# A two-layer block on one core: negated maxima, a later moments' copy, later subtractions, weight products from split operands

## The chip, the cores and the metric

The kernel runs on one core of one Trainium2 chip. The metric is the device time of one execution in microseconds; the median of three runs is given. TensorE (PE) multiplies matrices, VectorE (DVE), ScalarE (ACT) and GpSimd (POOL) work on elements, SyncE (SP) issues the DMAs. PEld is PE's loading of weights, recorded beside its products.

## The reference

The input x holds 4 batches of 512 tokens with 256 features. Each of two layers computes a mixing part s and a gate g from the same normalised input and adds their product:

```python
xn = layernorm(x)
x  = x + s(xn) * silu(ffn(xn))
```

The feed-forward part of both layers is `fwht(silu(xn @ W1.T) * (xn @ W3.T)) @ W2.T` with 1024 hidden features; `fwht` is a Walsh-Hadamard transform along them. In layer 0, s is a recurrence of one step from a zero state, so it is linear: `xn + rmsnorm(xn @ W_in.T * c @ W_out.T) * norm_w`, with c per channel. In layer 1, s is causal attention with one head: a second layernorm with gamma and beta, q, k, v, softmax of `q k.T / 16`, the product with v, an output projection, and xn added.

## The kernel before, in words

Products that must keep fp32's accuracy are made of split operands: `split` (L59 to L62) copies a tile to a rounded high part on ACT (type float32r, "f32r") and subtracts it from the original on DVE to get a low part. `mm3` (L80 to L87) then adds three products: high by high, high by low, low by high. So each split costs one ACT and one DVE instruction, and PE runs f32r products. A few products of weights run in native fp32 instead: `product_of_weights` (L179) makes M, the 256x256 mixing matrix of layer 0 (tile mps), the product wqk of the query and key weights divided by 16 (tile wqkps), and the product wvo of the value and output weights (tile wvops). In a trace a native product of 256 columns is two records.

The kernel treats one batch after another, first all four in layer 0, then all four in layer 1. A scheduler sets the order on each engine from costs and dependences; `after(ins)` adds a constraint that an instruction comes behind another.

Layer 0. The FFN of a batch (`ffn`, L450) goes through eight hidden blocks c of 128: the up products of W1 and W3 (tile f_0gu for batch 0: the digit in f_0 is the batch), silu on ACT (L511), the product h on DVE (L512), the split of h into hh and hl (L519), and the down product of an earlier block (tile f_0dn). Beside it a list of tasks is stepped through slots (`Beside`, L850), two per block: the mixer, the norm of the next batch, and preparations. For batch 0 all down products are deferred to the end, so the split h of blocks 0 to 3 are kept in tiles "early", and the weights still have to be loaded and split beside it (w from w13raw, w2 by `prep_w2` at L139, M by `prep_m`). Batch 1 has among its tasks W2 of layer 1 and `prep_second`, which loads qk and vo and makes wqk and wvo.

`prep_s` (L311) prepares a quarter of layer 1's up weights for a form of Strassen's product with seven products for eight: it loads sraw, makes four sums on DVE (ssum), splits both into sp, and stores them to DRAM in four DMAs. `load_s` (L334) loads them back as tiles sw whenever the FFN of layer 1 (`ffn_s`, L536) needs them, into the four slots of w13. The stores and loads are issued by SP in its own order, like all large transfers. Tiles of 512 KB share ten slots (t4, L44): sraw, ssum, sp, qk, vo, the split q k product tq, v, p and the moments.

Layer 1. `norm(1, b)` (L416) computes the layernorm of batch b, then the moments of a second one (`moments`, L240), transposes them on PE (tile mrp), copies the 8 rows on ACT (L431), writes them to DRAM (L433) and loads them back, broadcast to all partitions, as mrb (L435). `Attention` (L711) makes tq (L757) from the scaled input and wqk, v from wvo, and the scores sc (L775) for four tiles of 128 rows. For each tile the mask is added on DVE (L792), a maximum taken (nmax, L794) and multiplied by -1 (neg, L796). `soft` (L798) makes the four exponentials p on ACT with neg as bias (L807). The first of a batch is preceded by a load of ACT's function table, since silu was used before. `pt` (L814) transposes p on PE in three groups (tiles 0 and 1, tile 2, tile 3) and splits it into ph and pl; `pv` (L828) multiplies by v. In layer 1 the order of PE is written out by hand: a list `places` (from L1058 on) says which attention step goes beside which of the FFN's products.

Of the kernel before, what the change touches and what calls it, by code (L numbers as in the profile page):

```python
# [35 lines left out]
def kernel(ctx: ExitStack, tc: tile.TileContext, a: dict, out: bass.AP):  # L36
# [139 lines left out]
    def w2_tiles(layer):  # L176
        return w2_tile(f"w2h_{layer}"), w2_tile(f"w2l_{layer}")

    def product_of_weights(name, lhsT, rhs, nk, scale=None):  # L179
# [9 lines left out]
        if scale is None:  # L189
            split(o, hi, lo)  # L190
        else:
            nc.scalar.mul(hi, o, scale)
            nc.vector.scalar_tensor_tensor(lo, o, scale, hi.bitcast(F32), ALU.mult, ALU.subtract)
        return hi, lo

    def load_m():
# [24 lines left out]
    def sl(i):  # L221
        return slice(i * P, (i + 1) * P)
# [3 lines left out]
        nc.sync.dma_start(raw, a[name])  # L226
        return raw

    def prep_qk(qk):
        return product_of_weights(  # L230
            "wqk", lambda k, i: qk[:, 0, k, sl(i)], lambda k: qk[:, 1, k, :], 2, 1.0 / 16.0
        )

    def prep_vo(vo):
        return product_of_weights(
            "wvo", lambda k, i: vo[:, 0, k, sl(i)], lambda k: vo[:, 1, k, :], 2
        )


    def moments(name, x, mr):  # L240
# [175 lines left out]
    def norm(layer, b):  # L416
        xn = act.tile([P, NT, D], F32, tag="xn", name=f"xn{layer}_{b}", bufs=3)
        xns[layer, b] = xn
        with after(first["gate"] if b > 1 - layer else None):
            first["scaled"] = layernorm(f"ln{layer}_{b}", xs[b], xn)  # L420
        yield
        if layer:


            mr = act.tile([P, 2, NT], F32, tag="mr", name=f"mr{b}", bufs=2)
            moments(f"ln2_{b}", xn, mr)
            yield
# [3 lines left out]
            nc.scalar.copy(rows, o)  # L431
# [3 lines left out]
            nc.sync.dma_start(  # L435
                mrb, there.rearrange("(a t) p -> a (t p)", a=2).unsqueeze(0).to_broadcast([P, 2, S])
            )
# [12 lines left out]
    def ffn(name, xT, w13, w2, slot, defer=1, spare=(), parts=1, behind=False, tail=()):  # L450
# [30 lines left out]
                        ins = one(False)  # L481
            return ins

        queue, gates = [], []
        for c in range(NH):
            with after(gates[-2] if behind and c >= 2 else None):
                wh, wl = w13(c // 2)
            gu = []
            for j in range(2):

                o = psum(f"{name}gu{c}_{j}", [P, S], **(DN[0] if behind and c == 1 else GU))
                cols = slice((c % 2) * D + j * P, (c % 2) * D + (j + 1) * P)
                gu.append((o, cols))
            for half in range(parts if c == 0 else 1):
                n = S // (parts if c == 0 else 1)
                ts_ = slice(half * n, (half + 1) * n)
# [15 lines left out]
            gates.append(nc.vector.tensor_tensor(h, h, gu[1], ALU.mult))  # L512
            first["gate"] = gates[-1]
            if c < len(spare):
                hh, hl = spare[c]
            else:
                hh = hid(f"{name}hh{c}", F32R)
                hl = hid(f"{name}hl{c}", F32R)
            split(h, hh, hl)  # L519
            queue.append((c, hh, hl))  # L520
            ups = last_up if behind else None
            with after(gates[-1] if behind else None), after(ups):
                slot(2 * c)
            if len(queue) > defer:
# [186 lines left out]
    class Attention:  # L711
# [63 lines left out]
        def sc(self, i):  # L775

            b = self.b
            if i == 0:
                self.both = psum(f"sc{b}_0", [P, 2, 2 * P])
                self.scs = [self.both[:, 0, :], self.both[:, 1, :]]  # L780
                self.nmax, self.neg, self.den = (
                    act.tile([P, NT], F32, tag=n, name=f"{n}{b}", bufs=2) for n in ("nmax", "neg", "den")
                )
            elif i > 1:
                self.scs.append(psum(f"sc{b}_{i}", [P, S]))
# [5 lines left out]
            for t in ones:  # L791
                nc.vector.tensor_tensor(self.scs[t][:, sl(t)], self.scs[t][:, sl(t)], mask, ALU.add)  # L792
            for t in ones:
                nc.vector.reduce_max(self.nmax[:, t : t + 1], self.scs[t][:, : (t + 1) * P], AX.X)  # L794
            ts_ = slice(ones[0], ones[-1] + 1)
            nc.vector.tensor_scalar(self.neg[:, ts_], self.nmax[:, ts_], -1.0, None, ALU.mult)  # L796

        def soft(self):  # L798

            b, ins = self.b, first["table"]  # L800
            self.ps, self.prs = [], []
            ps_ = [t4(f"p{b}_{i}", [P, 2, S]) for i in range(2)]
            for i, sc in enumerate(self.scs):
                w = (i + 1) * P
                p = ps_[i // 2][:, i % 2, :]
                with after(ins):
                    ins = nc.scalar.activation(  # L807
                        p[:, :w], sc[:, :w], AF.Exp,
# [41 lines left out]
    class Beside:  # L850
# [24 lines left out]
        def finish(self):  # L875
            while self.step():
                pass

    def some(gen, n):

        for _ in range(n):
            next(gen)
            yield

    def run(f, *args):
        return lambda: f(*args)
# [73 lines left out]
    def prep_second():  # L960
        qk, vo = load_pair("qk"), load_pair("vo")
        yield
        first["wqk"] = prep_qk(qk)
        yield
        first["wvo"] = prep_vo(vo)
        yield


# [1 line left out]
    for b in range(B):  # L970
# [8 lines left out]
        if b + 1 < B:  # L979
            if b:  # L980
                load_x(b + 1)
            if b == 2:
                tasks.append((prep_s(1), 4))
            tasks.append((norm(0, b + 1), NORM))
        if b == 0:
            early = w2_tile("early0"), w2_tile("early1")
# [4 lines left out]
        if b == 1:  # L991
            raw2_1 = load_w2(1)
            w2_1 = w2_tiles(1)
            tasks.append((prep_w2(1, raw2_1, w2_1, t4), W2P))
            tasks.append((prep_second(), 3))
            tasks.append((prep_s(0), 4))
        if b == 2:
            tasks += [(prep_s(2), 4), (norm(1, 0), NORM), (prep_s(3), 4)]
        if b == 3:
            atts = [Attention(0)]  # L1000
            a = atts[0]
            parts = run(a.xt_half, 0), run(a.xt_half, 1), a.xt, a.scaled, a.split_sums
# [43 lines left out]
    for b in range(B):  # L1046
        a, final = atts[b], b + 1 == B
        sc, pv, v = ([run(f, i) for i in range(NT)] for f in (a.sc, a.pv, lambda i: a.v(i // 2, i % 2)))
        pts = [run(a.pt, *tiles) for tiles in ((0, 1), (2,), (3,))]
        adds, later_gates = {}, [lambda: None] * 2  # L1050
        if b:
# [7 lines left out]
        else:  # L1059
            places = [[[v[0]], [v[1]], [v[2]], [sc[0]], [], [sc[1]], [v[3]], []]]  # L1060
        if not final:
            if b:
                places[0][2].append(run(next, norms[b + 1]))
            rows = run(next, norms[b + 1])
            c = Attention(b + 1)
            tq, v_ = [run(c.tq, j) for j in range(2)], [run(c.v, 0, j) for j in range(2)]
            atts.append(c)
            places += [
                [
                    [sc[2]], [sc[3], rows, a.soft], [0], [pts[0]],  # L1070
                    [1, later_gates[0]], [pts[1], later_gates[1]], [2], [pv[0], pv[1], 3],
                ],
                [
# [9 lines left out]
        else:  # L1083
            later = [[(q, c, (2, 3)) for c in range(2)] for q in range(2)]
            places += [
                [[sc[2]], [sc[3], a.soft], [0], [pts[0]], [1, later_gates[0]], [pts[1], later_gates[1]], [], [pv[0], pv[1]]],
                [[pts[2]], [pv[2], 0], [], [pv[3]], [1], [later[0][0]], [], [later[0][1]]],
                [[later[1][0]], [later[1][1]], [], [0], [], [1], [], []],
            ]
# [69 lines left out]
```

## Time and profile before

| what | us |
|---|---|
| median of three runs (lowest, highest) | 364.55 (364.49, 364.83) |
| the profiled execution | 364.85 |
| span of its trace | 363.0 |
| PE busy, PEld busy | 354.9, 327.3 |
| DVE busy, ACT busy, POOL busy | 283.9, 195.7, 20.5 |
| DMA: bytes moved | 52.25 MB |

The granted clock of TensorE is 1.00 throughout. The profile names tiles without buffer numbers: sw stands for all of sw0_0_0, sw0_1_1 and so on, where the text needs the number (sw0_1_1 is the high part of the second load, for quarter 1). Line L70 is `in_line`, the helper that records every matmul, so matmuls are told apart by their tiles. A row of a chain is start, length, engine, tile, line and count; a row of a timeline has besides, in brackets, the idle time before it and who ended it. As matmuls overlap in a pipeline, the duration of one (0.28 us for 256 columns) is longer than the distance between two starts.

### The profile page before, as it was taken

What the parts mean: (1) busy time and instruction counts of PE and PEld (TensorE: products, weight loads), DVE (VectorE), ACT (ScalarE), POOL (GpSimd) and SP (SyncE); (2) the same over time, 40 slices, a digit from 0 to 9 for tenths busy, and PEclk for the clock granted to TensorE, in tenths of its full rate; (3) what the DMA queues carried; (4) which work ended last, traced back from release to release, by engine and by line L of the source; (5) the groups of instructions that cost most, each with busy time, mean ns of one, the idle gap of its engine ahead of it and who ended that gap; (6) DMA issues with size and microseconds to landing.
All of it is one profiled execution on the core that took longest, in us unless ns stands there. A gap on an engine that the chain in (4) does not pass through costs nothing.

```text
span 363.0 us, 6253 instructions
## 1 busy us (share of the span) xinstructions
PE 354.9 (98%) x2461; PEld 327.3 (90%) x2461; DVE 283.9 (78%) x602; ACT 195.7 (54%) x370; POOL 20.5 (6%) x22
## 2 busy tenths in 40 slices
PE   8999999999999999999999999999999999999995
PEld 6867998888988898888989999899999899999995
DVE  6898548997569938897787957979669898568646
ACT  3647526265373424663467655577653876446443
POOL 1000201000020210101100001100011000000000
PEclk9999999999999999999999999999999999999999
DMA  7924200414235416633057145662554645345401
GB/s 242 327 61 148 87 0 2 128 46 178 84 127 179 159 27 218 259 121 105 1 209 255 33 171 205 225 204 95 202 201 144 197 188 202 114 148 212 194 2 58
DMA packets 16285, 52.25 MB, mean 144 GB/s; under 512 B 1633, under 2 KB 7937, under 8 KB 16257
## 3 DMA queue, kind: packets, MB, share of 16 engines
q1 hardware_dynamic: 15968, 51.60, 40.1%
q8 instruction: 19, 0.31, 0.4%
q10 hardware_dynamic: 288, 0.26, 0.2%
q14 instruction: 10, 0.07, 0.1%
HBM read 42.40 MB, written 9.45 MB: 143 GB/s over the span
## 4 chain that ended last, share of the span: by engine, by line
PE 80%; DVE 15%; ACT 1%; issue 1%; DMA 1%; POOL 1%; DVEq 0%
PE f_1gu L70 6%; PE f_2gu L70 6%; PE f_3gu L70 6%; PE f_3dn L70 6%; PE f_2dn L70 6%; PE f_0dn L70 5%; PE f_1dn L70 5%; PE f_0gu L70 4%; PE pv L70 4%; PE tq L70 3%; PE o L70 3%; PE v L70 2%; PE sc L70 2%; PE mps L70 1%; PE pt L70 1%; DVE nmax L794 1%
## 5 line engine op out<-in xcount | busy, mean ns | idle before, releaser
L70 PE MATMUL f_0gu<-xt,w 128*128 128x512 f32 (+1 forms) x108 | 25.3, 383 | 0.6 <-DVE f_0h L512 0.5
L70 PE MATMUL f_3gu<-xt,w 128*128 128x512 f32 x96 | 25.0, 396 | 0.0
L70 PE MATMUL f_2gu<-xt,w 128*128 128x512 f32 x96 | 24.6, 395 | 0.0
L70 PE MATMUL f_1gu<-xt,w 128*128 128x512 f32 x96 | 24.5, 395 | 0.0
L70 PEld LDWEIGHTS f_0gu<-xt,w 128*128 128x128 f32 x108 | 18.3, 188 | 6.1 <-DVE f_0h L512 0.9
L70 PEld LDWEIGHTS f_1gu<-xt,w 128*128 128x128 f32 x96 | 17.2, 188 | 3.3
L70 PEld LDWEIGHTS f_2gu<-xt,w 128*128 128x128 f32 x96 | 17.1, 188 | 3.2
L70 PEld LDWEIGHTS f_3gu<-xt,w 128*128 128x128 f32 x96 | 17.0, 188 | 2.9
L61 ACT CAST f_1hh<-f_1h 128x512 fp32r<-128x512 f32 x16 | 9.9, 621 | 16.6 <-DVE f_1h L512 12.3
L61 ACT CAST f_2hh<-f_2h 128x512 fp32r<-128x512 f32 x16 | 9.9, 621 | 15.6 <-DVE f_2h L512 11.2
L70 PE MATMUL f_1dn<-w2l,f_1hh 128*128 128x256 f32 x64 | 17.9, 284 | 0.0
L70 PE MATMUL f_3dn<-w2l,f_3hh 128*128 128x256 f32 x64 | 17.7, 281 | 0.0
L70 PE MATMUL f_1dn<-w2h,f_1hh 128*128 128x256 f32 x64 | 17.7, 281 | 0.0
L70 PE MATMUL f_3dn<-w2h,f_3hh 128*128 128x256 f32 x64 | 17.7, 281 | 0.0
L70 PE MATMUL f_2dn<-w2h,f_2hh 128*128 128x256 f32 x64 | 17.7, 282 | 0.0
L70 PE MATMUL f_2dn<-w2l,f_2hh 128*128 128x256 f32 x64 | 17.6, 280 | 0.0
L70 PE MATMUL f_1dn<-w2h,f_1hl 128*128 128x256 f32 x64 | 17.3, 284 | 0.1
L70 PE MATMUL f_3dn<-w2h,f_3hl 128*128 128x256 f32 x64 | 17.0, 282 | 0.0
L70 PE MATMUL f_2dn<-w2h,f_2hl 128*128 128x256 f32 x64 | 16.8, 283 | 0.1
L61 ACT CAST f_3hh<-f_3h 128x512 fp32r<-128x512 f32 (+1 forms) x17 | 10.1, 596 | 12.1 <-DVE f_3h L512 7.9
L62 DVE TENSOR_TENSOR f_2hl<-f_2h,f_2hh 128x512 fp32r<-128x512 f32 x16 | 11.0, 686 | 4.8 <-ACT f_2hh L61 4.8
L62 DVE TENSOR_TENSOR f_3hl<-f_3h,f_3hh 128x512 fp32r<-128x512 f32 (+1 forms) x17 | 11.1, 656 | 3.6 <-ACT f_3hh L61 3.3
(469 smaller groups left out, 1137.9 us busy)
## 6 DMA issues: line engine op xcount, KB each, us to landing
sw<-s SPq DMA_DIRECT2D x32, 896.0 KB, 4.7
s<-sp SPq DMA_DIRECT2D x8, 512.0 KB, 3.4
s<-sp SPq DMA_DIRECT2D x8, 384.0 KB, 4.3
w2raw<-in_w SPq DMA_DIRECT2D x4, 512.0 KB, 6.3
sraw<-in_w SPq DMA_DIRECT2D x4, 512.0 KB, 4.6
mrb<-there SPq DMA_DIRECT2D x4, 512.0 KB, 3.9
w13raw<-in_w SPq DMA_DIRECT2D x3, 512.0 KB, 8.4
x<-in_x SPq DMA_DIRECT2D x3, 512.0 KB, 3.5
```

The source lines that it names most:

```text
L61: h = nc.scalar.copy(hi, src)
L62: return h, engine.tensor_tensor(lo, src, hi.bitcast(F32), ALU.subtract)
L70: ins = call(*args, **kwargs)
L794: nc.vector.reduce_max(self.nmax[:, t : t + 1], self.scs[t][:, : (t + 1) * P], AX.X)
```

## The change

It has five parts.

1. The maxima are written negated straight into neg; the tile nmax and the multiplication by -1 go (12 DVE instructions).
2. `soft` is cut into halves. `places` has the first half, the moments' copy, then the second half, and the copy is put behind the last exponential by `after`.
3. In batch 0 of layer 0 the blocks 0 to 3 make only the high part hh at once. The four subtractions for hl are collected in `late` and issued behind the products h of the blocks 6 and 7, two each.
4. wqk and wvo are made from split operands: qk and vo are split as whole tiles, and `product_of_pair` uses `mm3`. `prep_second` has five steps in place of three.
5. `prep_s` of quarters 0, 1, 2 moves from batches 1, 2, 2 to batch 2 in other places, and that of quarter 3 from batch 2 to batch 3. The first two steps of norm(1, 1) move from the tasks of batch 3 to layer 1: the layernorm to its start, the moments to the place where the other batches have them.

```diff
-    def prep_qk(qk):
-        return product_of_weights(
-            "wqk", lambda k, i: qk[:, 0, k, sl(i)], lambda k: qk[:, 1, k, :], 2, 1.0 / 16.0
-        )
...
+    def split_pair(name, raw):
+        parts = [t4(f"{name}{i}", [P, 2, 2, D], F32R) for i in "hl"]
+        split(raw, *parts)
+        return parts
+
+    def product_of_pair(name, parts, scale=None):
...
+        for i in range(2):
+            mm3(
+                o[:, i, :],
+                [
+                    (tuple(p[:, 0, k, sl(i)] for p in parts), tuple(p[:, 1, k, :] for p in parts))
+                    for k in range(2)
+                ],
+            )
...
-            nc.scalar.copy(rows, o)
+            with after(first["table"] if b else None):
+                nc.scalar.copy(rows, o)
...
-            split(h, hh, hl)
+            if c < len(spare):
+                nc.scalar.copy(hh, h)
+                late.append((hl, h, hh))
+            else:
+                split(h, hh, hl)
+            for _ in range(2 if c >= NH - 2 else 0):
+                if late:
+                    lo_, h_, hi_ = late.pop(0)
+                    with after(gates[-1]):
+                        nc.vector.tensor_tensor(lo_, h_, hi_.bitcast(F32), ALU.subtract)
...
-                nc.vector.reduce_max(self.nmax[:, t : t + 1], self.scs[t][:, : (t + 1) * P], AX.X)
-            ts_ = slice(ones[0], ones[-1] + 1)
-            nc.vector.tensor_scalar(self.neg[:, ts_], self.nmax[:, ts_], -1.0, None, ALU.mult)
+                nc.vector.reduce_max(
+                    self.neg[:, t : t + 1], self.scs[t][:, : (t + 1) * P], AX.X, negate=True
+                )
...
-        first["wqk"] = prep_qk(qk)
-        yield
-        first["wvo"] = prep_vo(vo)
+        qk = split_pair("qk", qk)
+        yield
+        vo = split_pair("vo", vo)
+        yield
+        first["wqk"] = product_of_pair("wqk", qk, 1.0 / 16.0)
+        yield
+        first["wvo"] = product_of_pair("wvo", vo)
...
             if b == 2:
-                tasks.append((prep_s(1), 4))
+                tasks.append((prep_s(0), 4))
             tasks.append((norm(0, b + 1), NORM))
...
-            tasks.append((prep_second(), 3))
-            tasks.append((prep_s(0), 4))
+            tasks.append((prep_second(), 5))
         if b == 2:
-            tasks += [(prep_s(2), 4), (norm(1, 0), NORM), (prep_s(3), 4)]
+            tasks += [(prep_s(1), 4), (norm(1, 0), NORM), (prep_s(2), 4)]
...
             norms = {1: norm(1, 1)}
-            tasks.append((some(norms[1], 2), 2))
+            tasks.append((prep_s(3), 4))
...
-            if b:
-                places[0][2].append(run(next, norms[b + 1]))
+            if b == 0:
+                next(norms[1])
+            places[0][2].append(run(next, norms[b + 1]))
...
-                    [sc[2]], [sc[3], rows, a.soft], [0], [pts[0]],
+                    [sc[2]], [sc[3], soft[0], rows, soft[1]], [0], [pts[0]],
```

More of the change, by code (lines that the diff above doesn't have):

```diff
@@ L177, in w2_tiles, with product_of_weights @@
         return w2_tile(f"w2h_{layer}"), w2_tile(f"w2l_{layer}")
-    def product_of_weights(name, lhsT, rhs, nk, scale=None):
+    def product_of_weights(name, lhsT, rhs, nk):
         hi = wp.tile([P, 2, D], F32R, name=f"{name}h")
@@ L188, in product_of_weights @@
                 )
[L189 to L193, printed above, removed]
+        split(o, hi, lo)
         return hi, lo
@@ L227, in load_pair @@
         return raw
-    def prep_qk(qk):
-        return product_of_weights(
-            "wqk", lambda k, i: qk[:, 0, k, sl(i)], lambda k: qk[:, 1, k, :], 2, 1.0 / 16.0
-        )
[L234 to L237, printed above, removed]
+    def split_pair(name, raw):
[3 more added lines that the diff above has]
+    def product_of_pair(name, parts, scale=None):
+        hi = wp.tile([P, 2, D], F32R, name=f"{name}h")
+        lo = wp.tile([P, 2, D], F32R, name=f"{name}l")
+        o = psum(f"{name}ps", [P, 2, D])
+        for i in range(2):
[6 more added lines that the diff above has]
+            )
+        if scale is None:
+            split(o, hi, lo)
+        else:
+            nc.scalar.mul(hi, o, scale)
+            nc.vector.scalar_tensor_tensor(lo, o, scale, hi.bitcast(F32), ALU.mult, ALU.subtract)
+        return hi, lo
     def moments(name, x, mr):
@@ L482, in down @@
             return ins
-        queue, gates = [], []
+        queue, gates, late = [], [], []
         for c in range(NH):
@@ L518, in ffn @@
                 hl = hid(f"{name}hl{c}", F32R)
-            split(h, hh, hl)
+            if c < len(spare):
+                nc.scalar.copy(hh, h)
+                late.append((hl, h, hh))
+            else:
+                split(h, hh, hl)
[4 more added lines that the diff above has]
+                        nc.vector.tensor_tensor(lo_, h_, hi_.bitcast(F32), ALU.subtract)
             queue.append((c, hh, hl))
@@ L780, in sc @@
                 self.scs = [self.both[:, 0, :], self.both[:, 1, :]]
-                self.nmax, self.neg, self.den = (
-                    act.tile([P, NT], F32, tag=n, name=f"{n}{b}", bufs=2) for n in ("nmax", "neg", "den")
+                self.neg, self.den = (
+                    act.tile([P, NT], F32, tag=n, name=f"{n}{b}", bufs=2) for n in ("neg", "den")
                 )
@@ L793, in sc, with soft @@
             for t in ones:
-                nc.vector.reduce_max(self.nmax[:, t : t + 1], self.scs[t][:, : (t + 1) * P], AX.X)
-            ts_ = slice(ones[0], ones[-1] + 1)
-            nc.vector.tensor_scalar(self.neg[:, ts_], self.nmax[:, ts_], -1.0, None, ALU.mult)
-        def soft(self):
+                nc.vector.reduce_max(
+                    self.neg[:, t : t + 1], self.scs[t][:, : (t + 1) * P], AX.X, negate=True
+                )
+        def soft(self, h):
             b, ins = self.b, first["table"]
-            self.ps, self.prs = [], []
-            ps_ = [t4(f"p{b}_{i}", [P, 2, S]) for i in range(2)]
-            for i, sc in enumerate(self.scs):
+            if h == 0:
+                self.ps, self.prs = [], []
+            half = t4(f"p{b}_{h}", [P, 2, S])
+            for i in (2 * h, 2 * h + 1):
+                sc = self.scs[i]
                 w = (i + 1) * P
-                p = ps_[i // 2][:, i % 2, :]
+                p = half[:, i % 2, :]
                 with after(ins):
@@ L877, in finish @@
                 pass
-    def some(gen, n):
-        for _ in range(n):
-            next(gen)
-            yield
     def run(f, *args):
@@ L994 @@
             tasks.append((prep_w2(1, raw2_1, w2_1, t4), W2P))
-            tasks.append((prep_second(), 3))
-            tasks.append((prep_s(0), 4))
+            tasks.append((prep_second(), 5))
         if b == 2:
-            tasks += [(prep_s(2), 4), (norm(1, 0), NORM), (prep_s(3), 4)]
+            tasks += [(prep_s(1), 4), (norm(1, 0), NORM), (prep_s(2), 4)]
         if b == 3:
             atts = [Attention(0)]
-            a = atts[0]
-            parts = run(a.xt_half, 0), run(a.xt_half, 1), a.xt, a.scaled, a.split_sums
+            at = atts[0]
+            parts = run(at.xt_half, 0), run(at.xt_half, 1), at.xt, at.scaled, at.split_sums
             tasks += [(call(f), 1) for f in parts]
             norms = {1: norm(1, 1)}
-            tasks.append((some(norms[1], 2), 2))
+            tasks.append((prep_s(3), 4))
         bg = Beside(*tasks)
@@ L1048 @@
         sc, pv, v = ([run(f, i) for i in range(NT)] for f in (a.sc, a.pv, lambda i: a.v(i // 2, i % 2)))
+        soft = [run(a.soft, i) for i in range(2)]
         pts = [run(a.pt, *tiles) for tiles in ((0, 1), (2,), (3,))]
@@ L1085 @@
             places += [
-                [[sc[2]], [sc[3], a.soft], [0], [pts[0]], [1, later_gates[0]], [pts[1], later_gates[1]], [], [pv[0], pv[1]]],
+                [[sc[2]], [sc[3], *soft], [0], [pts[0]], [1, later_gates[0]], [pts[1], later_gates[1]], [], [pv[0], pv[1]]],
                 [[pts[2]], [pv[2], 0], [], [pv[3]], [1], [later[0][0]], [], [later[0][1]]],
```

## The prediction, made before the result was known

> **What bounds the kernel now.** I read the page first: the share of each engine and the chain that ended last.
>
> ```profile
> PE 354.9 (98%) x2461; PEld 327.3 (90%) x2461; DVE 283.9 (78%) x602; ACT 195.7 (54%) x370; POOL 20.5 (6%) x22
> ...
> PE 80%; DVE 15%; ACT 1%; issue 1%; DMA 1%; POOL 1%; DVEq 0%
> ```
>
> PE sets the end. An edit gains only by taking away matmul time or a place where PE stands still, and loses only where it makes PE stand. The waits of PE by name are next (engine, tile and line, who was late; us in total, times, longest).
>
> ```profile
> PE warm L70 <- DVE zr L904: 1.4, 1, 1.4
> PE pt L70 <- ACT p L807: 1.4, 3, 0.5
> PE f_0gu L70 <- DVE f_0h L512: 0.5, 1, 0.5
> PE xt_0tp L70 <- DVE xn L390: 0.2, 1, 0.2
> PE f_0gu L70 <- DVE w L62: 0.2, 1, 0.2
> ```
>
> Three of these five touch the change: the transposes of p (three times) and the two f_0gu waits. The table of stretches shows where they lie (length, then busy us of PE, PEld, DVE, ACT, POOL).
>
> ```profile
> 20.00:30.00 10.00, 9.36 (x37) 6.36 (x36) 10.00 (x18) 4.84 (x10) 0.00 (x0) 1.00 0.34 105
> 30.00:40.00 10.00, 10.00 (x54) 8.67 (x53) 7.59 (x18) 5.62 (x11) 0.00 (x0) 1.00 0.44 158
> 60.00:80.00 20.00, 20.00 (x115) 17.32 (x114) 19.17 (x40) 9.34 (x19) 2.77 (x2) 1.00 0.26 79
> 160.00:180.00 20.00, 20.00 (x139) 18.55 (x138) 14.79 (x40) 8.83 (x15) 2.39 (x2) 1.00 0.26 90
> 180.00:190.00 10.00, 9.53 (x73) 8.97 (x72) 8.14 (x21) 6.10 (x15) 0.00 (x0) 1.00 0.52 186
> 230.00:240.00 10.00, 9.46 (x70) 8.69 (x69) 10.00 (x24) 7.11 (x17) 1.27 (x1) 1.00 0.80 286
> 280.00:290.00 10.00, 9.44 (x76) 8.80 (x75) 8.54 (x20) 7.65 (x16) 0.00 (x0) 1.00 0.72 230
> ```
>
> PE is short of full at 20 to 30, 180 to 190, 230 to 240 and 280 to 290, and nowhere else in these rows. Matmuls are pipelined, so busy time hides small stalls. I therefore counted start to start: in undisturbed runs one 256-column product on split operands (f32r) follows the last by 0.118 us, a 512-column one by 0.233. The timeline's starts beyond that spacing give the stalls below. All times are in the clock of the profiled execution (364.85 us, span 363.0), 0.30 above the median of the three runs (364.55). "New order" is the order in which the changed kernel's instructions stand on each engine, as its scheduler leaves them.
>
> **The weight products (wqk, wvo).** The chain has them, and mps, as (start, us):
>
> ```profile
> 30.97 3.45 PE mps L70 x16
> ...
> 90.61 1.73 PE wqkps L70 x8
> 92.33 1.73 PE wvops L70 x8
> ```
>
> Eight native fp32 matmuls are recorded as 16 passes of 0.216 each, 3.46 us, and the first f32r matmul behind a native block comes 0.19 later than its spacing. The new form is 24 f32r matmuls of 256 columns, 24 x 0.118 = 2.84 (the chain also shows 12 such o products in 1.43). So 3.46 + 0.19 - 2.84 gives -0.81 us. Added are two copies of 128x1024 on ACT (1.05 each) and two subtractions on DVE (interval 1.14 each, 2.3 in all). They stand in batch 1, where DVE has 0.83 idle in 20. Their cover is that the Strassen sums of quarter 0 (four adds at 0.34, two subtractions at 0.87 and 1.14: 3.4 us of DVE) leave batch 1 for batch 2, so DVE there loses 1.1 net. Uncovered, the 2.3 us in front of a subtraction that PE needs would eat the gain whole: from -0.81 to +1.5. I take -0.81, because the readers of that stretch's split parts stand later on PE in the new order, behind the next up products.
>
> **The first batch's subtractions.** DVE is full at 20 to 30. The four subtractions of early tiles start at 18.05, 19.25, 24.32 and 28.59, 0.60 each; three precede the product h4 (26.73) and the split of the last w13 quarter (27.33), for which PE waits at 27.46 and 28.60. Beyond the spacing, PE loses 0.26 at 23.95, 0.73 at 27.46 and 0.44 at 28.60, together 1.43. Without the three, both producers are 3 x 0.60 = 1.8 earlier, more than any of these waits. The four then take 2.4 us of DVE at 33 to 38, where 30 to 40 has 2.41 idle; their first reader is at 41.25. Their cover is thin: norm and splits of batch 1 come later by up to 1.5, and its first product, at 53.3, leaves room. Against this, the new order cuts the mps block into three pieces among up products, so the 0.19 behind a native block is paid twice more: +0.37. Walked instruction by instruction with these intervals, I get -0.84; ends -0.4 (one wait stays) and -1.06 (all goes).
>
> **The softmax.** ACT at layer 1's first batch (start, us, operation, idle before):
>
> ```profile
> 186.13 0.26 ACT L431 COPY rows<-mrp 8x128 f32<-8x128 f32 x1 [2.32 <-PE mrp L70]
> 186.40 1.28 ACT L807 ACT_TABLE_LOAD   x1
> 187.70 0.37 ACT L807 ACTIVATE p<-sc,neg 128x128 f32<-128x128 f32 x1
> 188.06 0.47 ACT L807 ACTIVATE p<-sc,neg 128x256 f32<-128x256 f32 x1
> ```
>
> ACT idles 2.32 for the moments' transpose, and only then loads the exponential's table. With the copy behind two exponentials, the load starts after the silu that ends at 183.81 and ends at 185.1; neg is there by 182.7. The exponentials end near 186, and PE asks for them at 188.2: its gap of 0.62 goes. Batches 1 and 2 have gaps of 0.60 and 0.62 at 235.75 and 283.38. In batch 1 neg (233.45) is what comes last then: 233.6 + 0.37 + 0.47 is 234.4, against 235.28. In both batches a second stall of 0.37 follows (239.82, 287.44), where a down product waits for a subtraction of h; that one moves ahead of an add on DVE in the new order, and I count it gone. In batch 0 the third exponential comes behind the copy of the transposed p, and I charge 0.2 for a late subtraction there. Sum: -0.45, -0.97, -0.99, or -2.4; ends -1.2 (second stalls stay, half of the first come back) and -2.6. The last batch had no wait. The copy, and with it the moments' round trip through DRAM, is up to 0.9 later; its consumers (tq) show waits of only 0.2 to 0.3, so I add nothing, with +0.5 as the end. The rule weighed here: the Trainium skill (ScalarE: Activation LUTs, What ACT_TABLE_LOAD costs) gives 2.66 us for a switch of table sets, a load of 1.28 and a drain of 1.38. The load here agrees (1.28); 0.02 us lies between it and the exponential, so no drain is paid behind it. If it were, batch 0 would still be in time (187.4 against 188.2), but batch 1 not surely.
>
> **Negated maxima.** Twelve tensor_scalar of 148 ns go, 1.8 us of DVE, three between a maximum and its exponential per batch. PE waits for none of these by name, so nothing, with -0.3 as the end.
>
> **The moved tasks.** The sums of quarter 3 move to the end of batch 3 and meet the norm of layer 1's batch 1. The idle DVE time of 160 to 180 (5.2 us) takes the 3.4. What worries me is their load. Now it runs at SP's 134.53, directly behind the moments' load, landing at 139.7:
>
> ```profile
> 134.13 0.34 SPq L435 DMA_DIRECT2D mrb<-there  x1
> 134.53 0.42 SPq L314 DMA_DIRECT2D sraw<-in_w  x1
> ```
>
> In the new SP order it stands behind sw0_1_1, which waits until up products have read their weights: about 159.7, so the load is issued at 160.1 and lands, 5.2 later, at L = 165.3. DVE runs in order. From L to the end of the subtraction hl7 stand ssum 3 x 0.34, hl6 0.60, ssum 0.34, sp0 0.87, h7 0.60, statistics 1.36, sp3 1.14, tql 0.60, two aggregates 0.2, hl7 0.60: 7.3 us. PE reads hl7 at 172.2, so it stands by L - 164.9 = 0.4. The page's other 512 KB loads bound it: sraw 4.6 by median (no stall), w2raw 6.3 (L = 166.4, 1.5), w13raw 8.4 (L = 168.5, 3.6). I take +0.4, from this same transfer's own row. A rule that speaks against the change: descriptors start in order within a queue on a DMA engine (the Trainium skill, DMA: Bandwidth & Descriptors, Issuing engines are not separate DMA queues). By it the load starts only when 896 KB of sw0_1_1 are read; 4.1 us for these and, at the same rate, 2.4 more for 512 KB make L = 166.2 and the stall 1.3 instead of 0.4, the sum -2.75 instead of -3.65. The row of 134.53 was itself issued 0.4 behind a load of 512 KB, so its 5.2 holds part of such a wait already.
>
> **Sum.** -0.81 - 0.84 - 2.4 + 0.4 = -3.65; 364.85 - 3.65 = 361.2 in the profiled clock, 360.9 from the median. I say 361.2, the later of the two, as waits that go tend to leave a smaller one behind.
>
> **The rivals.**
> Only half arrives (0.24). DVE is full where the second stalls lie (10.00 of 10 at 230 to 240), and the load costs 1.5, as w2raw's duration makes it. Then -0.81 - 0.6 - 1.4 + 1.5 is -1.3: 363.5; with the load at 0.4 it is 362.4. For it: full DVE, in-order queues. Against: the first-half exponentials come 0.85 or more ahead of need.
> Slower (0.08): the late load of quarter 3. Its stores to DRAM release slots that tql0, vl0, the first exponentials and the moments' load reuse, and its DVE work stands in front of the last up product's h7, hl7 and v0. Each us of lateness is a us of PE. It turns the sign when L passes 164.9 + 4.05 = 168.95, that is, when the load takes 8.9 from its issue, 0.5 more than w13raw's 8.4. At L = 170 the time is 365.9.
> No change (0.05): the mps switches and the batch-1 splits eat both weight terms (+0.7 in place of -0.81, -0.4) and the softmax gives 1.2, with the load at +1.5: 365.4; with the load at +0.4 it is 364.3.
>
> **Numbers.** Forecast 361.2, its own range 360.2 to 362.2, chance 0.63. The range of 8 in 10 reaches into the first rival: 360.1 to 363.6. About 0.2% (0.7 us) is what a measurement can tell from no change. Faster 0.87, within it 0.05, slower 0.08.
>
> **What would show it.** PE busy near 10.0 at 20 to 30 and in the three softmax stretches; no wait of pt for p; the table load directly behind a silu; wqkps as 12 matmuls in 1.42. Wrong would be: a DVE wait for sraw near 163 to 168 with PE waiting for hl7, vl or tq behind it; a new PE wait on a split in batch 1 (65 to 90); PE waiting for tq's operands in batches 1 and 2.

## The result, and the profile after

| | before | after |
|---|---|---|
| median (lowest, highest), us | 364.55 (364.49, 364.83) | 363.0 (362.72, 363.14) |
| profiled execution, its span | 364.85, 363.0 | 362.72, 360.9 |
| PE, PEld, DVE, ACT busy | 354.9, 327.3, 283.9, 195.7 | 354.3, 327.9, 286.1, 197.5 |

The ratio is 0.9956, its 95% interval 0.9941 to 0.997. The change makes the kernel 1.55 us faster. 3.35 were forecast (364.55 to 361.2), so less than half of it came, close to the first rival (362.4 to 363.5). All three waits of PE that the prediction aimed at are gone, and two others stand in the list, here of the changed kernel:

```profile
PE warm L70 <- DVE zr L921: 1.4, 1, 1.4
PE f_3dn L70 <- DVE f_3hl L62: 0.4, 1, 0.4
PE f_2dn L70 <- DVE f_2hl L62: 0.2, 1, 0.2
```

The stretches of the changed kernel, in the same columns as before and shifted by what it is earlier there:

```profile
20.00:30.00 10.00, 10.00 (x44) 7.91 (x43) 8.77 (x15) 5.56 (x11) 0.00 (x0) 1.00 0.32 107
...
158.00:178.00 20.00, 19.58 (x132) 17.81 (x131) 17.70 (x39) 10.46 (x18) 1.01 (x1) 1.00 0.58 212
178.00:188.00 10.00, 10.00 (x79) 9.64 (x78) 9.12 (x25) 5.07 (x11) 1.01 (x1) 1.00 0.51 186
228.00:238.00 10.00, 9.89 (x75) 9.30 (x74) 10.00 (x24) 6.66 (x16) 1.31 (x1) 1.00 0.75 258
278.00:288.00 10.00, 9.90 (x80) 9.32 (x79) 8.88 (x19) 6.38 (x16) 0.00 (x0) 1.00 0.71 240
```

PE is full where it had stalled at 20 to 30, and 19.58 of 20 where it had been full at the end of layer 0. Busy time still hides small stalls: it is 9.89 of 10 at 228 to 238, where starts are 0.37 late in all. So I took the start of the same matmul in both traces, counted from the first up product (f_0gu), and read off by which landmark how much was gained. This table is the base of all that follows; the columns are what a stage gained (minus) or lost:

| kernel | first f_0gu at | to first f_0dn | to f_2gu | to f_3gu | to layer 1 | its batch 0 | batch 1 | batch 2 | rest | sum |
|---|---|---|---|---|---|---|---|---|---|---|
| before | 7.89 | 0 | 0 | 0 | 0 | 0 | 0 | 0 | 0 | 0 |
| after | 7.67 | -1.43 | -0.01 | -0.03 | +0.76 | -0.13 | -0.68 | -0.41 | +0.05 | -1.88 |
| late_only | 7.63 | -1.43 | -0.01 | +0.01 | -0.01 | 0.00 | 0.00 | -0.05 | +0.02 | -1.47 |
| products_only | 7.78 | -0.32 | +0.02 | -0.07 | +0.03 | 0.00 | 0.00 | -0.04 | 0.00 | -0.37 |
| soft_only | 7.95 | +0.05 | +0.01 | 0.00 | 0.00 | -0.13 | -0.68 | -0.41 | +0.06 | -1.10 |
| tasks_back | 7.80 | -1.44 | -0.01 | -0.07 | +0.07 | -0.15 | -0.69 | -0.71 | +0.05 | -2.93 |
| no_products | 7.80 | -1.39 | -0.01 | +0.01 | -0.01 | -0.14 | -0.67 | -0.69 | +0.06 | -2.84 |
| load_early | 7.83 | -1.43 | +0.02 | -0.03 | +0.78 | -0.15 | -0.71 | -0.71 | +0.06 | -2.17 |
| load_early_order | 7.81 | -1.42 | -0.01 | -0.03 | +0.04 | -0.13 | -0.69 | -0.73 | +0.05 | -2.91 |
| norm_first | 7.73 | -1.46 | -0.01 | -0.58 | +1.68 | -0.14 | -0.67 | -0.67 | +0.06 | -1.78 |
| copy_act_back | 7.80 | -1.43 | -0.01 | -0.09 | +0.07 | -0.15 | -0.64 | -0.69 | +0.14 | -2.80 |
| hh_early_copy | 7.96 | -1.49 | -0.01 | -0.07 | +0.07 | -0.02 | -1.10 | -0.87 | +0.13 | -3.36 |
| sums_behind | 8.00 | -1.49 | 0.00 | -0.58 | +0.07 | -0.14 | -0.67 | -0.73 | +0.06 | -3.49 |
| both | 8.03 | -1.51 | +0.01 | -0.58 | +0.07 | 0.00 | -1.10 | -1.22 | +0.14 | -4.19 |
| two_batches | 7.55 | -1.29 | 0.00 | -0.58 | +0.07 | -0.15 | -1.12 | -1.18 | +0.05 | -4.20 |

The first column differs by up to 0.48 us although nothing ahead of that product was changed, so totals of single executions carry that much chance; before's profiled execution stood 0.30 above its median, after's 0.28 below. The stages agree between kernels to within 0.07 where the code is the same, except for the first: its waits for DVE were worth 1.43 in before's execution, 1.1 in that of products_only and 1.5 in that of soft_only, all with the same code there.

### The profile page after: what moved, and what is told of

Same layout as the page of the kernel before. It is cut to its first block, busy times and chain, and to the rows that moved or that the text cites. A ratio compares the mean times of both kernels' runs of the same rounds, so it can differ in the third digit from the quotient of the medians.

```text
span 360.9 us, 6262 instructions
## 1 busy us (share of the span) xinstructions
PE 354.3 (98%) x2469; PEld 327.9 (91%) x2469; DVE 286.1 (79%) x592; ACT 197.5 (55%) x372; POOL 19.0 (5%) x22
## 4 chain that ended last, share of the span: by engine, by line
PE 78%; DVE 16%; ACT 2%; DMA 1%; issue 1%; POOL 1%; DVEq 0%; SPq 0%; ACTq 0%
PE f_0gu L70 6%; PE f_1gu L70 6%; PE f_0dn L70 5%; PE f_2dn L70 5%; PE f_3dn L70 5%; PE f_1dn L70 5%; PE f_3gu L70 5%; PE pv L70 4%; PE f_2gu L70 3%; PE tq L70 2%; PE o L70 2%; PE v L70 2%; PE sc L70 2%; PE warm L70 2%; DMA sraw<-in_w 1%; DVE sp L62 1%
## 5 line engine op out<-in xcount | busy, mean ns | idle before, releaser
L70 PE MATMUL f_0dn<-w2h,f_0hl 128*128 128x256 f32 x48 | 13.7, 284 | 0.1
```

Source lines behind the costliest of these rows:

```text
L70: ins = call(*args, **kwargs)
```

## The experiments

My theory was at each point the one called A in the expectations. Every number below is from the table or from the run's own trace.

**late_only**: before, with the late subtractions alone.

```diff
-            split(h, hh, hl)
+            if c < len(spare):
+                nc.scalar.copy(hh, h)
+                late.append((hl, h, hh))
...
```

> The kernel before with the late subtractions of batch 0 alone. Here too the mps block is cut into three pieces. Theory A (a native block costs nothing where it meets products on split operands, since its last pass is followed after 0.03 us and the next product after 0.42, together the usual 0.45; the stalls of 1.43 all go): the first down product starts 1.4 earlier, time about 363.1. Theory B (the prediction on record: two more switches at 0.19 each): 0.84 to 1.05 earlier, 363.5 to 363.7.

Measured: 363.4 (363.11 to 363.57), ratio 0.9968 (0.9956 to 0.9981). The first down product starts 1.43 earlier, with the mps block in three pieces. The time alone would not decide, as 363.4 lies nearer to B's 363.5 than to A's 363.1, and the stage's waits differ between executions. The starts decide. Here is where a native block ends, once in the kernel before and once in late_only:

```profile
33.61 0.81 PE L70 MATMUL mps<-wg,win 128*128 128x256 f32 x3
34.07 1.05 PE L70 MATMUL f_0gu<-xt,w 128*128 128x512 f32 x3
...
26.34 0.59 PE L70 MATMUL mps<-wg,win 128*128 128x256 f32 x2
26.58 1.05 PE L70 MATMUL f_0gu<-xt,w 128*128 128x512 f32 x3
```

With 0.216 from pass to pass the last one starts at 34.04 and at 26.56. The next product follows 0.03 later and the one behind it after 0.42, 0.45 in all, as 0.216 + 0.233. All three borders of mps in late_only read so, and in the rest of the stage no product waits 0.1 or more. I had counted the second distance and not the first. A holds, B's price for switches falls.

**products_only**: before, with wqk and wvo from split operands alone (the diff's `split_pair`, `product_of_pair` and `prep_second` with five steps, tasks as before).

> The kernel before with the wqk and wvo products from split operands alone, prep_second in five steps, the other tasks where they were. Theory A (16 passes of 0.216 become 24 products of 0.119, no switch): PE 0.58 to 0.60 earlier behind wvops and no new stall, time about 364.0. Theory B (on record): 0.81 earlier, 363.7. Rival C (the two splits of 128x1024 overfill DVE in batches 1 and 2, as the sums of quarter 0 stay there): a new wait for a subtraction between 65 and 120 of 0.3 or more, time 364.3 or later.

Measured: 364.34 (364.21 to 364.74), ratio 0.9996 (0.9987 to 1.0005): no difference. The products themselves are cheaper, as the chain of the changed kernel shows:

```profile
88.37 1.43 PE wqkps L70 x12
89.80 1.42 PE f_1dn L70 x12
91.22 1.44 PE wvops L70 x12
```

1.43 + 1.44 in place of 3.46 is 0.59 less. It is lost again at 115.4 in products_only. This is DVE there, in order:

```profile
111.77 1.20 DVE L723 TENSOR_TENSOR xn<-xn,osb 128x1024 f32<-128x1024 f32 x1
112.90 0.41 DVE L334 TENSOR_TENSOR ssum<-sraw 128x256 f32<-128x256 f32 x1
113.23 0.41 DVE L335 TENSOR_TENSOR ssum<-sraw 128x256 f32<-128x256 f32 x1
113.57 0.24 DVE L278 BATCH_NORM_AGGREGATE ln_3mv<-ln_3st 128x2 f32<-128x6 f32 x2
113.73 0.92 DVE L62 TENSOR_TENSOR sp<-sraw,sp 128x768 fp32r<-128x768 f32 x1
...
114.73 0.65 DVE L62 TENSOR_TENSOR f_2hl<-f_2h,f_2hh 128x512 fp32r<-128x512 f32 x1
```

and the same stretch before:

```profile
113.12 1.21 DVE L708 TENSOR_TENSOR xn<-xn,osb 128x1024 f32<-128x1024 f32 x1
114.25 0.24 DVE L263 BATCH_NORM_AGGREGATE ln_3mv<-ln_3st 128x2 f32<-128x6 f32 x2
114.40 0.66 DVE L62 TENSOR_TENSOR f_2hl<-f_2h,f_2hh 128x512 fp32r<-128x512 f32 x1
114.98 0.42 DVE L319 TENSOR_TENSOR ssum<-sraw 128x256 f32<-128x256 f32 x1
```

Before, f_2hl follows directly behind xn. With split products the scheduler puts two sums and a subtraction of a quarter (0.34 + 0.34 + 0.84) ahead of it, and PE waits 0.48 beyond its spacing. So rival C's time (364.3 or later) and its wait for a subtraction came true, but not its reason: where the splits stand no wait comes (+0.02 to the first f_2gu), and what changed is the order 20 us later.

**soft_only**: before, with the negated maxima and the split `soft` alone (the diff's parts 1 and 2).

> The kernel before with the negated maxima and the moments' copy behind two exponentials, nothing else. Theory A (DVE is full in these stretches, so each transposes' wait of 0.6 goes but a wait of about 0.37 for a copy or subtraction on DVE takes the place of the old second one): batches 0, 1, 2 give 0.3, 0.65 and 0.4, together 1.3 to 1.4, time about 363.2. Theory B (on record: the second stalls go as well): 2.4, time about 362.1.

Measured: 363.36 (363.1 to 363.79), ratio 0.9971 (0.996 to 0.9982). 0.13, 0.68 and 0.41 in the three batches, 1.22, the very numbers of the changed kernel. B falls; A is right in kind and 0.1 to 0.2 too large. ACT in the changed kernel shows that the part does what it says:

```profile
182.29 0.59 ACT L600 ACTIVATE f_0h<-f_0gu0g 128x512 f32<-128x512 f32 x1
182.90 1.28 ACT L830 ACT_TABLE_LOAD   x1
184.20 0.37 ACT L830 ACTIVATE p<-sc,neg 128x128 f32<-128x128 f32 x1
184.46 0.19 ACT L830 ACTIVATION_READ_ACCUMULATOR p<-sc,neg 128x1 f32 x1
184.56 0.46 ACT L830 ACTIVATE p<-sc,neg 128x256 f32<-128x256 f32 x1
```

The table is loaded directly behind the silu, and p is there 2 us before PE asks for it.

**tasks_back**: the changed kernel with part 5 undone.

```diff
-                tasks.append((prep_s(0), 4))
+                tasks.append((prep_s(1), 4))
...
             tasks.append((prep_second(), 5))
+            tasks.append((prep_s(0), 4))
...
-            tasks += [(prep_s(1), 4), (norm(1, 0), NORM), (prep_s(2), 4)]
+            tasks += [(prep_s(2), 4), (norm(1, 0), NORM), (prep_s(3), 4)]
...
-            tasks.append((prep_s(3), 4))
+            tasks.append((some(norms[1], 2), 2))
...
```

> The changed kernel with the tasks of part 5 where they were before (quarters 0 to 3 and the norm of layer 1's batch 1), the other four parts kept. Theory A (the moved tasks cost a wait for a subtraction of batch 2 of 0.48, a wait of 0.69 behind the late load of quarter 3, and a tq wait of 0.3 in layer 1's batch 0): all three go, the last product starts 1.2 to 1.5 earlier than in the changed kernel, time about 361.7. Rival C (the moved tasks are the cover of the splits of qk and vo, and without the move DVE makes PE wait in batches 1 to 3 by about as much): time 362.7 to 363.3.

Measured: 361.78 (361.66 to 362.1), ratio 0.9926 (0.9913 to 0.994): 1.2 better than the changed kernel and near A's 361.7; the last product starts 1.05 earlier by the table, a little under A's 1.2. But of A's three waits only the 0.69 for f_3hl went with the tasks. The 0.48 for f_2hl stays (it belongs to the products), the tq wait in batch 0 stays (soft_only has it too), and a tq wait in batch 2 went that I had not put down to the tasks (-0.71 in place of -0.41). Rival C's wait doesn't come: part 5 costs about 1 us, and the cover that I had given it for the splits isn't needed, as the stage to f_2gu is the same with and without it.

**no_products**: tasks_back with wqk and wvo in native fp32, as before.

> The kernel tasks_back with wqk and wvo in native fp32 as before, so the later subtractions, the negated maxima and the later copy alone. Theory A (the split products give 0.6 and cost 0.48 by putting the sums of a quarter ahead of a subtraction in batch 2, which comes only from the order): no wait in batch 2, 0.6 later at the end of wvops, and at the end within 0.25 of tasks_back, 361.7 to 362.1. Theory B (the products are worth what was on record): 362.4 to 362.6.

Measured: 361.76 (361.58 to 361.9), ratio 0.9924 (0.9912 to 0.9937), and 361.78 with them. A holds: the products are worth nothing here as they stand.

**load_early**: the changed kernel with quarter 3's load issued at the start of batch 3.

```diff
+            third = prep_s(3)
...
-            tasks.append((prep_s(3), 4))
+            next(third)
+            tasks.append((third, 3))
```

> The changed kernel, but the load of quarter 3 (sraw) is issued at the start of batch 3, ahead of sw0_1_1 on SP, its sums where they were in the changed kernel. Theory A (the wait of 0.69 for the last subtraction of batch 3 is the late landing at 163.7): no wait for sraw on DVE and none for f_3hl on PE, layer 1 starts 0.65 earlier, time about 362.3 to 362.5. Rival C (the 3.4 us of sums are too much for DVE at the end of batch 3 wherever the load stands): PE still waits 0.4 or more for f_3hl, time 362.8 to 363.1.

Measured: 362.56 (362.48 to 362.98), ratio 0.9948 (0.9936 to 0.9961). The time is near the one that A named, but not for A's reason: the stage to layer 1 is at +0.78 as in the changed kernel, with the wait of 0.69 for f_3hl that C expected, and the gain is the tq wait of batch 2. DVE no longer waits for sraw, and yet f_3hl comes at 170.78. ACT of load_early says why:

```profile
167.11 0.59 ACT L61 CAST tqh<-tq 128x512 fp32r<-128x512 f32 x1 [0.51 <-ACT f_3h L523]
169.40 0.59 ACT L61 CAST tqh<-tq 128x512 fp32r<-128x512 f32 x1 [1.70 <-PE tq L70]
169.88 0.62 ACT L61 CAST f_3hh<-f_3h 128x512 fp32r<-128x512 f32 x1
```

The scheduler put the last f_3hh behind a copy that waits for PE.

**load_early_order**: load_early, with the splits of tq behind that copy.

```diff
...
-            split(o, self.tqs[0][:, j, :], self.tqs[1][:, j, :])
+            with after(first["hh"] if b == 0 else None):
+                split(o, self.tqs[0][:, j, :], self.tqs[1][:, j, :])
...
```

> The kernel load_early, where the load of quarter 3 was early but the last copy f_3hh stood behind both copies of tq on ACT, with one edit more: the splits of tq come behind that copy. Quarter 3's sums then stand on DVE ahead of the last product of batch 3, none waits for a load, and only 1.4 of statistics stands before the last subtraction. Theory A (in the changed kernel the late landing pushed 1.5 us of idle time into a full DVE queue): no wait for f_3hl, layer 1 starts 0.65 earlier than in the changed kernel, time 361.9 to 362.1. Rival C (the sums alone are too much there): a wait of 0.3 or more stays for f_3hl, tq or v, 362.3 or later.

Measured: 361.84 (361.75 to 362.18), ratio 0.9925 (0.9913 to 0.9938). The stage to layer 1 is at +0.04, with all of quarter 3's sums still at the end of batch 3. So A: the sums fit there when their load is early and the order is kept. In the changed kernel the load makes the end of layer 0 late, as the chain of the stretch from 160 to 175 shows:

```profile
158.48 5.35 DMA sraw<-in_w
...
163.95 0.42 DVE ssum L330
...
168.76 1.12 DVE sp L62
169.88 0.60 DVE tql L62
170.48 0.15 DVE ln_1mv L274 x2
170.64 0.59 DVE f_3hl L62
171.23 0.04 issue
171.27 1.46 PE f_3dn L70 x10
```

**norm_first**: tasks_back with the norm ahead of quarter 2, so that f_2hl stands first on DVE.

```diff
-            tasks += [(prep_s(2), 4), (norm(1, 0), NORM), (prep_s(3), 4)]
+            tasks += [(norm(1, 0), NORM), (prep_s(2), 4), (prep_s(3), 4)]
```

> The kernel tasks_back with the norm of layer 1's batch 0 ahead of quarter 2 in the tasks of batch 2; on DVE the subtraction f_2hl then stands ahead of that quarter's sums. Theory A (the order on DVE made the wait of 0.48): no wait for f_2hl, 0.45 earlier behind batch 2; if the sums of quarters 2 and 3, now later, find idle DVE in batch 3, the time is about 361.3. Rival C (DVE work is only pushed on): a wait of 0.4 or more for a subtraction or a load in batch 3, time 361.7 or later.

Measured: 362.92 (362.4 to 363.9), ratio 0.9961 (0.9948 to 0.9975). The wait for f_2hl goes (-0.58), and 1.68 comes back in batch 3. The waits of PE in norm_first:

```profile
PE f_3dn L70 <- ACT f_3hh L61: 0.5, 1, 0.5
PE tq L70 <- DVE xgl L62: 0.5, 1, 0.5
```

Both theories are right about their part; C about the time.

**copy_act_back**: tasks_back with the copy of z on ACT.

```diff
-            copy(h1, z)
+            nc.scalar.copy(h1, z)
```

> The kernel tasks_back with the copy of z (h1, second quarter of the Strassen product) on ACT instead of DVE. Theory A (in layer 1's batches 1 and 2 DVE is the bound behind the transposes of p: its copies and maxima stand in a full queue, and ACT is idle for 2.2 us there): 0.6 less on DVE, the waits of 0.37 of f_1gu1g and f_2gu1g go, time about 361.1. Theory B (PE waits there for the exponentials on ACT): the copy on ACT makes ph and the third exponential later, the waits stay or grow, 361.7 or later.

Measured: 361.93 (361.8 to 362.32), ratio 0.9932 (0.9918 to 0.9945): no gain. Neither theory holds whole. In the changed kernel DVE was late with the copy of f_1gu1g that PE's next product (at 236.17, 0.27 late) overwrites:

```profile
233.65 0.67 DVE L636 COPY f_1h<-f_1gu1z 128x512 f32<-128x512 f32 x1
234.24 0.68 DVE L700 TENSOR_TENSOR x<-x,g_0g 128x512 f32<-128x512 f32 x1
234.84 0.68 DVE L815 TENSOR_REDUCE neg<-sc 128x1 f32<-128x512 f32 x1
235.44 0.67 DVE L639 COPY f_1v<-f_1gu1g 128x512 f32<-128x512 f32 x1
```

With the first of these on ACT that wait goes, and the old one for f_1hl is back (0.37, at 237.48). On ACT its f_1hh stands behind ph and two exponentials, as copy_act_back shows:

```profile
234.00 0.48 ACT L61 CAST ph<-pt 128x384 fp32r<-128x384 f32 x1 [1.16 <-PE pt L70]
234.37 0.59 ACT L830 ACTIVATE p<-sc,neg 128x384 f32<-128x384 f32 x1
...
234.94 0.69 ACT L830 ACTIVATE p<-sc,neg 128x512 f32<-128x512 f32 x1
...
235.60 0.62 ACT L61 CAST f_1hh<-f_1h 128x512 fp32r<-128x512 f32 x1
```

On DVE of the same run a sum then goes ahead of the subtraction f_1hl, though hh is there at 236.22:

```profile
236.14 0.69 DVE L651 TENSOR_TENSOR f_1h<-f_1gu1g,f_1h 128x512 f32<-128x512 f32 x1
236.75 0.68 DVE L62 TENSOR_TENSOR f_1hl<-f_1h,f_1hh 128x512 fp32r<-128x512 f32 x1
```

**hh_early_copy**: copy_act_back, with f_hh no longer held behind the last exponential.

```diff
-                with after(copied), after(first["table"]):
+                with after(copied):
                     what()
```

> The kernel tasks_back with two edits in layer 1: the copy of z (h1) on ACT, as in copy_act_back, and the copy hh of the first quarter's second half no longer held behind the last exponential, so that it runs in ACT's idle 2.2 us ahead of the transposes' copy. Theory A (after the transposes PE waits for a chain through both engines: full DVE makes the copy of f_1gu1g late, and on ACT hh stands behind ph and two exponentials, so taking away one shows the other): both waits of batches 0 to 2 go, 0.37 each; with new tq waits of up to 0.25 each in return, time 360.8 to 361.3. Rival C (DVE has no time left in these stretches, so every wait comes back at the next reader): 361.6 or later.

Measured: 361.58 (361.32 to 361.7), ratio 0.9916 (0.9902 to 0.9929), later than A's range and at the edge of C's. Batches 1 and 2 behave as A says (-1.10, -0.87, with a tq wait of 0.30 in batch 2), but batch 0 gains a wait of 0.76, in the list as "f_0gu2z <- DVE f_0h".

**sums_behind**: tasks_back with quarter 2's first sums behind the subtraction of the moment.

```diff
-        nc.vector.tensor_tensor(s1, a21, a22, ALU.add)
-        nc.vector.tensor_tensor(s3, a11, a21, ALU.subtract)
+        with after(first["low"] if q == 2 else None):
+            nc.vector.tensor_tensor(s1, a21, a22, ALU.add)
+            nc.vector.tensor_tensor(s3, a11, a21, ALU.subtract)
...
```

> The kernel tasks_back with one constraint more: in batch 2 the sums of quarter 2 come behind the subtraction f_2hl that they stood ahead of. Theory A (the 0.48 in batch 2 is the order on DVE alone, and the gain of the split products is there to be had): no wait for f_2hl, 0.45 earlier to the end, time about 361.35. Rival C (work pushed on makes a wait in batch 3, as norm_first showed): a new wait of 0.3 or more there, 361.7 or later.

Measured: 361.32 (361.21 to 361.64), ratio 0.991 (0.9895 to 0.9925). A: -0.58 in that stage and nothing given back. The split products' gain was there.

**both**: sums_behind and hh_early_copy together.

> The edits of hh_early_copy and sums_behind together on tasks_back. Theory A: the two gains lie in different layers and add: 0.45 in batch 2 and 0.5 to 1.0 in layer 1, time 360.4 to 360.9, below every kernel so far. Rival C (waits move on): no better than the better of the two.

Measured: 360.75 (360.5 to 360.81), ratio 0.9892 (0.9879 to 0.9906). They add, as A said, and the tq wait that hh_early_copy had in batch 2 is gone besides (-1.22 for -0.87).

**two_batches**: both, with the two layer 1 edits in batches 1 and 2 alone.

```diff
+                with after(copied), after(None if b in (1, 2) else first["table"]):
...
+            (nc.scalar.copy if b in (1, 2) else copy)(h1, z)
```

> The kernel both, with the two layer 1 edits (copy of z on ACT, hh ahead of the exponentials) in batches 1 and 2 alone. Theory A (the softmax gain of a batch that did not arrive was eaten by ACT's hh behind two exponentials and DVE's late copy; in batch 0 a different order of DVE, with the product h0 behind the scaling of the output, made the new wait of 0.76 for f_0gu2z): batch 0 keeps its waits of 0.43 and 0.27 and loses that of 0.76, batches 1 and 2 keep none but about 0.1, the end 0.0 to 0.4 earlier than in both, time 360.3 to 360.75. Rival C (the waits of batches 1 and 2 are tied to what batch 0 does, through the load of the moments or of sw): one of the waits for f_1gu1g, f_2gu1g or their subtractions comes back with 0.3 or more, time 361.0 or later.

Measured: 360.38 (360.31 to 360.48), ratio 0.9883 (0.9867 to 0.99), the fastest kernel here. Its waits of PE are these:

```profile
PE warm L70 <- DVE zr L928: 1.5, 1, 1.5
PE f_0dn L70 <- DVE f_0hl L62: 0.2, 1, 0.2
```

Batches 1 and 2 give -1.12 and -1.18 whatever batch 0 does (-1.10 and -1.22 in both), so they are independent. The sums of the table are level (4.20, 4.19), but the first stage, where the code is the same, gave 0.22 less in this execution. In layer 1 two_batches gains 0.22 more than both, of it 0.15 in batch 0 and 0.09 in the rest; the medians are 0.37 apart, and 0.15 of that stays unexplained.

## Why the prediction was wrong, point by point

The sum on record was -3.65. By the table it is -1.88.

- **The softmax: -2.4 forecast, -1.22 measured.** This is the step that failed most. The three waits for p go as described. What failed is "a second stall of 0.37 follows ... that one moves ahead of an add on DVE in the new order, and I count it gone". The subtraction was moved, and the copy of f_1gu1g behind the maxima became the late one in its place, by the same 0.37. I had looked for the next late instruction on the engine that had been late, and not at what a full DVE (10.00 of 10 at 230 to 240 before and at 228 to 238 after; for batch 2 of the changed kernel, 10.00 at 272 to 282) would be late with once PE came 0.6 earlier. hh_early_copy and two_batches show that two queues held that point, DVE's and ACT's; batches 1 and 2 then give 2.3 together. In batch 0 the charge of 0.2 for a late subtraction was 0.37 (0.43 in other executions), and a tq wait of 0.26 came, which I had given nothing. The late subtraction there (f_0hl, 190.38) stands on DVE behind a sum that had waited for PE, though its hh was ready at 189.87. The moments' round trip, for which the range had up to 0.5, isn't what is late: in the changed kernel its load lands at 192.27 in batch 0 and is first read at 199.24.
- **The weight products: -0.81 forecast, -0.03 to the start of f_3gu measured.** The step "I take -0.81, because the readers of that stretch's split parts stand later" was about batch 1, and there it is right. The size was 0.59, since the 0.19 of the switch does not exist. The loss came in batch 2, where the changed order put a quarter's sums ahead of f_2hl. I had read the new order around the splits and not everywhere it had changed.
- **Quarter 3: +0.4 forecast, +0.76 measured.** The mechanism was right and on record, and f_3hl was the reader that waited: 0.58 itself, and 0.11 more to the product behind it. The other 0.07 tasks_back has too. The DVE work in between was sized right (163.95 to 171.23 is 7.28, 7.3 on record). Mis-sized were three small terms: the load landed 5.35 after its issue (5.2 taken), the first sum came 0.12 behind the landing, and the 0.11 behind a late product had no term (together 0.38, where 0.29 was missing). The rule that descriptors start in order stands in the Trainium skill on the page DMA: Bandwidth & Descriptors, in the section "Two DMAs through the same engine are not ordered" and not in the one that the prediction names. The trace agrees with it: the packets of this load begin at 161.7 in the changed kernel, the last of the 896 KB ahead of it at 161.9. But they took 1.7 us and not 2.4, so the stall of 1.3 estimated by it was too long. The moved tasks cost about 1 us in all and brought none of the cover that I counted for them.
- **The first batch's subtractions: -0.84 forecast, -1.43 measured.** What failed is "the 0.19 behind a native block is paid twice more: +0.37", by late_only. Without it the walk's own sum is -1.21, which lies within the 1.1 to 1.5 that these waits were worth in different executions (1.15 between the medians of before and late_only).
- **Negated maxima:** priced at nothing. Not run alone, so it stays within soft_only.

With these differences (subtractions, products, softmax, quarter 3), -3.65 - 0.59 + 0.78 + 1.18 + 0.36 is -1.92, which meets the -1.88. The chances put 0.24 on "only half arrives" and its reason, full DVE and in-order queues. Its reason was right for the softmax (-1.4 there, -1.22 measured), and I gave it too little: the row with DVE at 10.00 stood in the text. That its time came true as well (362.4 to 363.5) is in part luck, since it took the products 0.78 too high and the subtractions 0.83 too low.

What stays open: why batch 0 of layer 1 gives no more than 0.15 in any kernel (either its waits of 0.43 and 0.27 or one of 0.76), and what removes the tq wait of batch 2 in tasks_back and brings it back in hh_early_copy. In that batch DVE stands idle for a copy of tb on ACT ahead of f_2v, 0.29 in the changed kernel and 0.31 in hh_early_copy, and not in tasks_back; but copy_act_back has a tq wait of 0.25 without that idle time. The order on DVE and ACT that load_early_order sets was not run with the late load, nor the earlier hh without the copy on ACT.

## What to carry to other kernels

A stall that goes on the bounding engine is worth only what the next full queue allows: where a second engine is busy to the last tenth over the stretch, list its instructions in order up to the next few readers, and price the gain by those. When a scheduler sets the order, an edit is paid for wherever the order differs, here 20 us behind it, so compare the whole order of every engine and look at what stands ahead of each subtraction or copy that the bounding engine reads. And read an experiment by the stage it was made for: load_early had the expected time without the expected effect.

## What the runs showed of the hardware

A native fp32 product beside split ones costs no more than its passes: the last pass is followed after 0.03 us, and the next product after 0.42, or after 0.31 where a product of 256 columns stands behind it. That is the sum of the two usual distances, at all three borders of mps in the changed kernel and at those of mps and wvops before. The load of ACT's function table took 1.28 us each of eight times in the changed kernel, with 0.02 us of idle time ahead of it and 0.01 behind, so a switch cost 1.31 in all. The first up product starts between 7.55 and 8.03 us in 15 profiled executions whose code up to there is the same. A load of 512 KB issued 0.4 us behind one of 896 KB landed 5.35 after its issue, near the 5.2 of the same load behind one of 512 KB.
